# Layer 0 of a four-layer fp32 convolution net: who copies the expansion, when staged loads are used, and in what order the last convolution walks its cells

## The chip, the cores and the metric

The kernel runs on one core of one Trainium2 chip. The metric is the device time of one execution in microseconds (us), as the median of several runs. A difference below about 0.2% (14 us) can't be told from no change here.

## The reference, cut to what matters

Four layers, each of them `x + conv(group_norm(x))`, on `x` of shape (4, 64, 256, 256) in float32. Only layer 0 is changed:

```python
def _L0_conv_ref(x, w_in, w_dw, fft_filter, w_out):
    x = einsum('bchw,oc->bohw', x, w_in)               # 64 -> 384 channels (1x1)
    x = irfft2(rfft2(8x8 patches of x) * fft_filter)   # per channel, per patch
    x = depthwise_conv3x3(x, w_dw)                     # over patch borders
    x1, x2 = split(x, 2, axis=1)
    x = gelu(x1) * x2                                  # 192 channels
    return einsum('bchw,oc->bohw', x, w_out)           # 192 -> 64 channels (1x1)

x = x + _L0_conv_ref(_gn(x), ...)                      # _gn: group norm, 32 groups
```

## The kernel before, in words

**The mathematics.** The FFT filter on a patch and the 3x3 convolution after it are both linear and per channel, so the kernel turns them, for each channel, into one small matrix from the cells of a patch (and its right, lower and lower-right neighbours) to the cells of an output patch. These matrices are built once, at the start, and kept in DRAM (`wts`).

**The blocks.** The image is cut into 12 blocks `p` (4 images, 3 strips of 11 rows of patches each). A block is worked in four quarters `kb` of 96 channels. A quarter has these stages, in this order on TensorE (PE):

1. `expand(p, kb, t)` for 11 or 12 rows of patches `t`: 32 matmuls (64 rows in the trace, since each fp32 matmul is two instructions) of line 443 write one PSUM tile `psu`. Three copies then move it to the SBUF tile `u`: ScalarE (ACT) copies 128 partitions (line 452), then 64 partitions go once by ACT and once by VectorE (DVE) in turn over `t` (line 454), then DVE copies 64 more (line 455). The two halves of `u` hold even and odd patches at shifted places: E1, O1 are the places of the even and odd patch columns on the lower 64 partitions, O2, E2 on the upper.
2. `unit()`: one of the eight projections `project(p - 1, r)` of the block before, the last 1x1 convolution. Its operand `g` was written to DRAM by the block before and is loaded by `load_unit`: one residual tile `r` (two DMAs), and tiles `g1` and `g6` in two halves (some 12 DMAs), all issued by SyncE (SP). 32 matmuls (64 rows of the trace) in lines 585 and 592 write a PSUM tile `po`; DVE adds it to the residual (599, 601), takes statistics (607), and GpSimd (POOL) stores it (611).
3. `convolve(p, kb, g)` for `g` = 0 to 11: matmuls of lines 486 and 495 read `u` and weights `w`, and write a PSUM tile `pc`. ACT applies gelu into a tile `h` (502), DVE multiplies by the other half (503), POOL stores `h` to DRAM (506). One tile `w` serves two convolutions. After `g` = 6 a second `unit()` comes.

All PSUM tiles of the layer (`psu`, `pc`, `po`) are four banks wide and take turns in two slots (`quad`).

**What sets the order.** Everything stands in a manual schedule: PE, DVE, ACT and SP execute in the order in which the code is written, each waiting on its own operands. So a load at SP that waits for a free buffer holds back every load written after it, and an instruction of DVE or ACT that waits for a load holds back the copies written after it.

**The staged loads.** Beside `w`, `g` and `r`, two more streams come through SP within the quarters:

- Quarters 0 to 2 load pieces of the next image for its group-norm statistics: `load_stats` after each `g` with `g % 3 == 2`, `next_stats` (two statistics instructions of DVE, line 322) after each `g` with `g % 3 == 1`. The tiles have a pool of two buffers (`l0st`).
- Quarter 3 loads the input rows of the next block: `load_x` for two rows ahead of the convolutions 0 and 1, then `normalize_x` (ACT, line 258) of row `k` after the convolution `k + 1`, followed by the load of row `k + 2`. This pool has two buffers too (`l0x`).

`load_w` (line 463) is called ahead of every second convolution for the tile three places on; its pool has four buffers. The tiles `h` have three.

**At the start** SP loads statistics pieces in a pool of seven, then seven input rows, then the weights `win`, `wo6`, `wo1` (lines 656 to 658), two more rows, three tiles `w`; the last rows follow in the loop that normalizes.

**The projection's operands.** A row of `g` (34 values) holds 17 even and 17 odd patch columns, one after the other. The output must have them interleaved. `moving` reads them interleaved (innermost step from E1 to O1 or back, count 2), for one output cell `q` per matmul, and `out` is contiguous:

```python
return bass.AP(tensor=g.tensor, offset=g.offset + lo * CW + o, ap=[g.ap[0], [CW, m], [1, 8], [step, 2]])
out = lambda q, s: po[halves[s], q // 2, n * (q % 2) : n * (q % 2 + 1)].rearrange(
    "p (i j x) -> p i j x", i=m, x=2)
```

Of the kernel before, what the change touches and what calls it, by code (L numbers as in the profile page):

```python
# [10 lines left out]
F32 = mybir.dt.float32  # L11
# [6 lines left out]
C = 64  # L18
HID = 192
# [102 lines left out]
class _Net:  # L122
# [154 lines left out]
    def _layer0(self, ctx, dst):  # L277
        tc, nc, a, B, H, W = self.tc, self.nc, self.a, self.B, self.H, self.W
# [18 lines left out]
        NR = 11  # L297
# [9 lines left out]
        NB, NI = len(blocks), len(blocks) // B  # L307

        cp = pool("l0c", 1)
        p_xn, p_x, p_st = pool("l0xn", NR + 1), pool("l0x", 2), pool("l0st", 2)  # L310
        p_w, p_h = pool("l0w", 4), pool("l0h", 3)
        dr = ctx.enter_context(tc.tile_pool(name="l0d", bufs=1, space=DRAM))
        p_g = ctx.enter_context(tc.tile_pool(name="l0g", bufs=2, space=DRAM))
        wts = [dr.tile([2, 64, 2, Q, NC], F32, name=f"wt{t}") for t in range(HID // C)]
# [101 lines left out]
        def load_x(row, p_x=p_x):  # L416
            b, i = row
            x0[row] = p_x.tile([128, P, HW2], F32, tag="x", name=f"x0_{b}_{i}")
            for s in range(2):
                nc.sync.dma_start(x0[row][halves[s]], a["x"][b, :, P * i : P * i + P, s * HW2 : (s + 1) * HW2])  # L420
# [13 lines left out]
        def expand(p, kb, t):  # L434

            b, i0 = blocks[p]
            ps = quad(f"psu_{p}_{kb}_{t}")
            xn = xns[b, i0 + t]
            for k in range(2):
                for m in range(4):  # L440
                    for s in range(2):
                        for odd in range(2):
                            nc.tensor.matmul(  # L443
                                ps[halves[1 - odd], 2 * s + k, 2 * PB * m : 2 * PB * (m + 1)],
                                xn[halves[s], 2 * (4 * k + m) + odd].rearrange("p r w -> p (r w)"),
                                win[halves[s], kb, PB * (1 - odd) : PB * (3 - odd)], start=True, stop=True,
                            )
            v = ps[:, :, 0 : 8 * PB].rearrange("p s (m c) -> p c s m", m=4)
            n = 4 * 4
            at = lambda h, o: u[h, :, t * CW + o : t * CW + o + n].rearrange("p c (s m) -> p c s m", s=4)  # L450
            first, second = v[:, 0:PB], v[:, PB : 2 * PB]
            nc.scalar.copy(at(slice(0, 128), 1), first)  # L452
            lo, hi = halves
            (nc.vector.tensor_copy if t % 2 else nc.scalar.copy)(at(hi, E2 + 1), second[lo])  # L454
            nc.vector.tensor_copy(at(lo, O1), second[hi])  # L455

        def load_w(j):

            p, k = divmod(j, HID // 8)
            if p >= NB:  # L460
                return
            w = wl[j] = p_w.tile([128, 2, 4, NC], F32, tag="w", name=f"w_{j}")
            nc.sync.dma_start(
                w, wts[k // 8][:, :, :, 4 * (k % 8) : 4 * (k % 8) + 4].rearrange("h i k c n -> (h i) k c n")
            )
# [96 lines left out]
        def project(p, r):  # L562

            b, i0 = blocks[p]
            lo, hi, j0, rr = rows_in(p, r)
            m = hi - lo
            po = quad(f"po_{p}_{r}")
            rt = rts.pop((p, r))
            n = m * 16

            def moving(g, q, s):
                d = q < 7
                o, step = (O1 + 8 * s, E1 + 1 - O1) if d else (E1 + 8 * s, O1 - E1)
                return bass.AP(
                    tensor=g.tensor, offset=g.offset + lo * CW + o, ap=[g.ap[0], [CW, m], [1, 8], [step, 2]]
                )

            out = lambda q, s: po[halves[s], q // 2, n * (q % 2) : n * (q % 2 + 1)].rearrange(
                "p (i j x) -> p i j x", i=m, x=2
            )  # L580
            for half in range(2):
                g1, g6 = loads.pop((p, r, half))
                for q in range(4 * half, 4 * half + 4):
                    for s in range(2):
                        nc.tensor.matmul(  # L585
                            out(q, s), wo1, moving(g1[:, q % 4], q, s), start=(q % 2 == 0), stop=False,
                            skip_group_check=True,
                        )
                for q in (0, 2, 1, 3):
                    for s in range(2):  # L590
                        k = q // 2
                        nc.tensor.matmul(  # L592
                            out(4 * half + q, s), wo6[halves[k]], moving(g6[halves[k], q % 2], 4 * half + q, s),
                            start=False, stop=True, tile_position=(k * C, s * C), skip_group_check=True,
                        )
            rv = rt.rearrange("p i (j w) -> p w (i j)", w=P)
            pv = po[:, :, 0 : 2 * n].rearrange("p b (k n) -> p b k n", k=2)
            v = rv[:, 1:7].rearrange("p (b k) n -> p b k n", k=2)
            nc.vector.tensor_add(v, v, pv[:, 0:3])  # L599
            v = bass.AP(tensor=rv.tensor, offset=rv.offset + 7, ap=[rv.ap[0], [-7, 2], rv.ap[2]])  # L600
            nc.vector.tensor_add(v, v, pv[:, 3])  # L601
            if b not in bst1:
                bst1[b] = (self.stats_tile(f"bst1_{b}", 72), count())
            bst, slot = bst1[b]
            for k in range(0, m, 4):
                v = rt[:, k : min(k + 4, m)].rearrange("p i w -> p (i w)")
                nc.vector.bn_stats(bst[:, next(slot), :], v)
            if p % NI == NI - 1 and r == P - 1:
                self.norms.append(self.group_norm_parts(1, b, bst))
            for s in range(2):  # L610
                nc.gpsimd.dma_start(xr(dst[b])[rr][:, j0 : j0 + m, s * HW2 : (s + 1) * HW2], rt[halves[s]])  # L611

        def load_stats(b, j):
            t = st[b, j] = p_st.tile([128, 4, W], F32, tag="st", name=f"st{b}_{j}")
            for s in range(2):
                nc.sync.dma_start(t[halves[s]], src_t[b, :, j, s])

# [12 lines left out]
        with ordered:  # L630
# [6 lines left out]
            def first_stats(k):  # L637
# [2 lines left out]
                t = parts[k] = p_s.tile([128, 4, W], F32, tag="x", name=f"st_{k}")  # L640
                nc.sync.dma_start(t.rearrange("p r w -> p (r w)"), flat[:, 4 * W * k : 4 * W * (k + 1)])

            for k in range(7):
                first_stats(k)
            copies = [nc.scalar.copy, nc.gpsimd.tensor_copy, nc.scalar.copy]
# [6 lines left out]
            rows = rows_of(0)  # L652
            for row in rows[:7]:
                load_x(row, p_s)
            for s in range(2):
                nc.sync.dma_start(win[halves[s]], a["w_in"].rearrange("c (k n) -> c k n", k=4))
                nc.sync.dma_start(wo6[halves[s]], a["w_out"][128:HID])
            nc.sync.dma_start(wo1, a["w_out"][0:128])
            for row in rows[7:9]:
                load_x(row)  # L660
            for j in range(3):
                load_w(j)
            self.group_norm(0, 0, bst0, avgs)
            for k, row in enumerate(rows):
                normalize_x(row)
                if 7 <= k < 9:
                    load_x(rows[k + 2])
            ctx_a.close()

            p_1, p_6 = (pool(n, 2, side="right") for n in ("l0g1", "l0g6"))  # L670
# [13 lines left out]
            for p in range(NB + 1):  # L684
# [32 lines left out]
                for kb in range(4):  # L717
                    for t in range(NR + 1):
                        if 0 <= i0 + t < NP:
                            expand(p, kb, t)  # L720
                    unit()
                    for g in range(NG):
                        G = NG * kb + g
                        if g % 2 == 0:
                            load_w(p * (HID // 8) + G // 2 + 3)
                        if kb == 3 and g < 2 and g < len(fresh):
                            load_x(fresh[g])
                        convolve(p, kb, g)
                        self.next_norms()
                        if g == NG // 2:  # L730
                            unit()
                        if kb < 3:
                            if g % 3 == 2 and nk:
                                k = nk.pop(0)
                                load_stats(b + 1, k)
                                loaded.append(k)
                            if g % 3 == 1 and loaded:
                                next_stats(b + 1, loaded.pop(0))
                        else:
                            for k in loaded[:1]:  # L740
                                next_stats(b + 1, loaded.pop(0))
                            if 0 <= g - 1 < len(fresh):
                                k = g - 1
                                normalize_x(fresh[k])
                                if k + 2 < len(fresh):
                                    load_x(fresh[k + 2])
                for row in rows:
                    if row not in after:
                        xns.pop(row)
# [726 lines left out]
```

## Time and profile before

| | |
|---|---|
| median of 3 runs | 6848.48 us (6843.42 to 6849.02) |
| the profiled execution, its own time | 6848.19 us |
| span of its instructions | 6846.4 us |
| mean granted TensorE clock | 0.943 |
| PE busy | 5944.0 us, 87% |
| DVE busy | 3941.4 us, 58% |
| ACT busy | 2907.2 us, 42% |
| layer 0 (first `psu` matmul to last `po` matmul) | 114.5 to 4286.2 us |
| DMA, mean over the span | 212 GB/s |

How to read it. The profile holds one execution. Every row of its timeline is an instruction with its start, its length, its engine and its source line, the tiles written and read, and, in brackets, how long the engine had been idle before it and which event ended the idle time. PEld is the load of the stationary operand, which runs beside PE. SPq is a DMA issue. A table of windows gives, for a stretch of time, the busy time of each engine, the clock granted to PE, the share of 16 DMA engines in use, and GB/s. [...]

### The profile page before, as it was taken

The page shows a single profiled execution, that of the slowest core. Times are in us where ns is not written, and L with a number is a line of the kernel's source. Part 1 is how long each engine was busy: PE and PEld are TensorE (multiplying, and loading weights), DVE is VectorE, ACT ScalarE, POOL GpSimd, SP SyncE. Part 2 cuts the span into 40 slices and gives each one's busy share as a digit, 9 for nine tenths or more (in the row PEclk, how much of TensorE's full clock was granted, in tenths as well). Part 3 has the DMA queues.
Part 4 walks back from the last instruction along what each step waited for, and adds up shares of the span by engine and source line. Part 5 has one row for each costly group of instructions (what it writes and reads, how often), then busy time and mean ns, then how long its engine had stood idle before and what let it go on. Part 6 is the DMA issues. An engine that isn't in the chain of part 4 may idle for free.

```text
span 6846.4 us, 251669 instructions
## 1 busy us (share of the span) xinstructions
PE 5944.0 (87%) x115416; PEld 3058.7 (45%) x115416; DVE 3941.4 (58%) x4164; ACT 2907.2 (42%) x2900; POOL 1049.2 (15%) x1646
## 2 busy tenths in 40 slices
PE   2888888888888888888888886999989999999988
PEld 1444444444444444444444443333344444444476
DVE  5445444445444545444444343899878889886355
ACT  3333323232323233323333330677777788774211
POOL 3111111111111111111111111111112222221011
PEclk9999999999999999999999997999999999999855
DMA  7477878687878787878676768999956667667889
GB/s 221 147 197 200 215 201 220 196 216 198 213 202 212 205 214 200 209 207 209 176 207 174 206 176 220 242 228 228 230 132 174 171 175 176 176 168 253 333 342 395
DMA packets 878550, 1448.53 MB, mean 212 GB/s; under 512 B 77252, under 2 KB 586452, under 8 KB 875444
## 3 DMA queue, kind: packets, MB, share of 16 engines
q1 hardware_dynamic: 725284, 923.09, 53.4%
q0 software_dynamic: 148672, 500.14, 22.0%
q8 instruction: 908, 14.88, 1.0%
q10 hardware_dynamic: 3536, 9.20, 0.5%
q14 instruction: 150, 1.23, 0.1%
HBM read 932.08 MB, written 500.04 MB: 209 GB/s over the span
## 4 chain that ended last, share of the span: by engine, by line
PE 65%; DMA 13%; issue 7%; DVE 6%; ACT 5%; SPq 2%; POOL 1%; ACTq 0%; DVEq 0%; POOLq 0%
PE pc L495 12%; PE m L861 10%; PE pc L486 8%; PE one L1102 8%; PE psu L443 7%; PE div L1061 6%; DMA x<-in_x_dram 4%; PE po L585 4%; DVE u L455 3%; ACT u L452 3%; DMA g<-g 3%; DMA st<-in_x_dram 2%; PE psz L1091 2%; PE po L592 2%; DMA x<-x 2%
## 5 line engine op out<-in xcount | busy, mean ns | idle before, releaser
L443 PE MATMUL psu<-win,xn 64*64 64x96 f32 x34816 | 912.0, 258 | 507.3 <-DVE u L455 309.2
L503 DVE TENSOR_TENSOR h<-h,pc 128x748 f32<-128x748 f32 x576 | 536.2, 931 | 1248.5 <-ACT h L502 1248.4
L495 PE MATMUL pc<-u,w 64*16 64x374 f32 (+2 forms) x27648 | 1248.0, 484 | 0.0
L502 ACT ACTIVATE h<-pc 128x748 f32<-128x748 f32 x576 | 456.5, 793 | 1808.4 <-PE pc L495 1673.6
L443 PEld LDWEIGHTS psu<-win,xn 64*64 64x64 f32 x34816 | 825.2, 143 | 616.2 <-ACT u L452 203.9
L486 PE MATMUL pc<-u,w 64*64 64x374 f32 x9216 | 894.4, 497 | 81.4 <-DVE h L503 73.0
L495 PEld LDWEIGHTS pc<-u,w 64*16 64x16 f32 (+2 forms) x27648 | 413.8, 92 | 772.5 <-issue 772.3
L452 ACT COPY u<-psu 128x768 f32<-128x768 f32 x544 | 461.9, 849 | 665.1 <-PE psu L443 664.0
L506 POOL DMA_DIRECT2D g<-h x576 | 416.2, 723 | 1797.9 <-DVE h L503 1665.2
L258 ACT ACTIVATE xn<-x,nb,r 128x1024 f32<-128x1024 f32 (+3 forms) x272 | 486.4, 1791 | 459.7 <-DMA x<-in_x_dram 313.5
L455 DVE COPY u<-psu 64x768 f32<-64x768 f32 x544 | 521.7, 959 | 247.5 <-ACT u L454 238.0
L1047 DVE TENSOR_TENSOR q<-xn 128x2313 f32<-128x2313 f32 (+2 forms) x256 | 628.0, 2496 | 1.7 <-ACT xn L258 1.7
L1102 PE MATMUL one<-z,wp 32*32 32x512 f32 x16384 | 592.4, 596 | 19.1 <-issue 14.3
L486 PEld LDWEIGHTS pc<-u,w 64*64 64x64 f32 x9216 | 324.2, 134 | 588.4 <-issue 447.4
L1048 ACT ACTIVATE q<-q 128x2313 f32<-128x2313 f32 (+2 forms) x256 | 528.9, 2086 | 32.2 <-DVE q L1047 31.2
L1061 PE MATMUL div<-q,ones 64*32 64x512 f32 x8192 | 466.2, 594 | 13.6 <-ACT q L1048 9.3
L1102 PEld LDWEIGHTS one<-z,wp 32*32 32x32 f32 x16384 | 367.4, 103 | 225.9 <-issue 84.8
L454 DVE COPY u<-psu 64x768 f32<-64x768 f32 x272 | 258.9, 952 | 328.1 <-ACT u L452 327.1
L585 PE MATMUL po<-g,wo 128*64 128x176 f32 (+1 forms) x3072 | 360.1, 380 | 91.9 <-DMA g<-g 50.6
L1135 POOL DMA_DIRECT2D x<-r x512 | 274.5, 544 | 971.9 <-DVE r L1132 956.3
L611 POOL DMA_DIRECT2D x<-r x192 | 148.5, 778 | 1785.8 <-DVE r L601 1192.3
L599 DVE TENSOR_TENSOR r<-r,po 128x1056 f32<-128x1056 f32 (+1 forms) x96 | 197.3, 2055 | 367.4 <-PE po L592 335.6
(155 smaller groups left out, 6042.1 us busy)
## 6 DMA issues: line engine op xcount, KB each, us to landing
g<-h POOLq DMA_DIRECT2D x576, 374.0 KB, 7.3
x<-x SPq DMA_DIRECT2D x240, 640.0 KB, 6.5
w<-wt SPq DMA_DIRECT2D x288, 448.0 KB, 7.6
x<-x SPq DMA_DIRECT2D x100, 1024.0 KB, 14.1
g<-g SPq DMA_DIRECT2D x414, 187.0 KB, 5.7
g<-g SPq DMA_DIRECT2D x736, 93.5 KB, 5.5
x<-in_x_dram SPq DMA_DIRECT2D x256, 256.0 KB, 7.3
x<-o POOLq DMA_DIRECT2D x128, 512.0 KB, 8.3
```

Of the source, the lines that this page charges most:

```text
L443: nc.tensor.matmul(ps[halves[1 - odd], 2 * s + k, 2 * PB * m : 2 * PB * (m + 1)], xn[halves[s], 2 * (4 * k + m) + odd].rearrange("p r w -> ...
L452: nc.scalar.copy(at(slice(0, 128), 1), first)
L455: nc.vector.tensor_copy(at(lo, O1), second[hi])
L486: nc.tensor.matmul(out(C * c, C, k, h), w[halves[h], k, 2 * (G % 2) + c, 0:C], cells(h, 4 * g + 2 * k + c, 0, 0), start=True, stop=False, ...
L495: nc.tensor.matmul(out(q, m, k, h), w[halves[h], k, 2 * (G % 2) + c, c0 : c0 + m], cells(h, 4 * g + 2 * k + c, down, right), start=False, ...
L503: nc.vector.tensor_mul(h, h, v[:, 1])
L585: nc.tensor.matmul(out(q, s), wo1, moving(g1[:, q % 4], q, s), start=(q % 2 == 0), stop=False, skip_group_check=True,)
L861: nc.tensor.matmul(rows2(m)[halves[j], s], w[dx][halves[s]], ts[n][halves[s], i, 2 * j : 2 * j + 2, dx : dx + W], start=(dx == 0), stop=(d ...
L1047: nc.vector.tensor_sub(d, p0, p1)
L1048: nc.scalar.activation(d, d, AF.Square)
L1061: ins = nc.tensor.matmul(ps[quarters[j], h], ones[halves[h]], q[n, g, k][halves[h], r + 2 * j : r + 2 * j + 2, o : o + W], start=(m == 0), ...
L1102: ins = nc.tensor.matmul(rows2(ps[g])[quarters[j], k], w[quarters[i]], z[quarters[i], h, 2 * j + dy : 2 * j + dy + 2, dx : dx + W], tile_p ...
```

## The change

Six edits, all in layer 0.

1. The third copy of `expand` is no longer done in turn: ACT copies 28 of 48 channels, DVE the other 20, after DVE's own copy.
2. The pools: input rows and statistics pieces share one pool of four buffers; `w` has three buffers and is loaded two places ahead; `h` has four buffers.
3. Statistics pieces are loaded at `g % 3 == 0` and used two loads later.
4. Input rows of the next block: four are loaded at the end of quarter 2, each further one after the normalization of the row four before it.
5. In `project`, a matmul takes the cells of one parity `x` (even or odd patch columns) of two output cells `q`: its operand is read in runs of eight contiguous values and its output has step 2 in PSUM. The number of matmuls and their sizes stay.
6. At the start, the weights are loaded ahead of the first statistics pieces, four input rows follow the first seven at once, and two tiles `w` are loaded instead of three.

```diff
-        p_xn, p_x, p_st = pool("l0xn", NR + 1), pool("l0x", 2), pool("l0st", 2)
-        p_w, p_h = pool("l0w", 4), pool("l0h", 3)
+        p_xn, p_x = pool("l0xn", NR + 1), pool("l0x", 4)
+        p_w, p_h = pool("l0w", 3), pool("l0h", 4)
...
             nc.scalar.copy(at(slice(0, 128), 1), first)
             lo, hi = halves
-            (nc.vector.tensor_copy if t % 2 else nc.scalar.copy)(at(hi, E2 + 1), second[lo])
+            k = PB * 7 // 12
+            nc.scalar.copy(at(hi, E2 + 1)[:, 0:k], second[lo, 0:k])
             nc.vector.tensor_copy(at(lo, O1), second[hi])
+            nc.vector.tensor_copy(at(hi, E2 + 1)[:, k:], second[lo, k:])
...
-            def moving(g, q, s):
-                d = q < 7
-                o, step = (O1 + 8 * s, E1 + 1 - O1) if d else (E1 + 8 * s, O1 - E1)
+            def moving(g, bank, s, x):
+                at = lambda q: (O1 + 8 * s, E1 + 1 + 8 * s)[x] if q < 7 else (E1 + 8 * s, O1 + 8 * s)[x]
+                o, d = at(2 * bank), at(2 * bank + 1) - at(2 * bank)
                 return bass.AP(
-                    tensor=g.tensor, offset=g.offset + lo * CW + o, ap=[g.ap[0], [CW, m], [1, 8], [step, 2]]
+                    tensor=g.tensor, offset=g.offset + lo * CW + o, ap=[g.ap[0], [L + d, 2], [CW, m], [1, 8]]
                 )
 
-            out = lambda q, s: po[halves[s], q // 2, n * (q % 2) : n * (q % 2 + 1)].rearrange(
-                "p (i j x) -> p i j x", i=m, x=2
-            )
+            out = lambda bank, s, x: po[halves[s], bank, 0 : 2 * n].rearrange(
+                "p (q i j x) -> p x q i j", q=2, i=m, x=2
+            )[:, x]
             for half in range(2):
                 g1, g6 = loads.pop((p, r, half))
-                for q in range(4 * half, 4 * half + 4):
-                    for s in range(2):
-                        nc.tensor.matmul(
-                            out(q, s), wo1, moving(g1[:, q % 4], q, s), start=(q % 2 == 0), stop=False,
-                            skip_group_check=True,
-                        )
-                for q in (0, 2, 1, 3):
-                    for s in range(2):
-                        k = q // 2
-                        nc.tensor.matmul(
-                            out(4 * half + q, s), wo6[halves[k]], moving(g6[halves[k], q % 2], 4 * half + q, s),
-                            start=False, stop=True, tile_position=(k * C, s * C), skip_group_check=True,
-                        )
+                for k in range(2):
+                    for x in range(2):
+                        for s in range(2):
+                            nc.tensor.matmul(
+                                out(2 * half + k, s, x), wo1, moving(g1[:, 2 * k], 2 * half + k, s, x),
+                                start=(x == 0), stop=False, skip_group_check=True,
+                            )
+                for x in range(2):
+                    for k in range(2):
+                        for s in range(2):
+                            nc.tensor.matmul(
+                                out(2 * half + k, s, x), wo6[halves[k]],
+                                moving(g6[halves[k], 0], 2 * half + k, s, x),
+                                start=False, stop=True, tile_position=(k * C, s * C), skip_group_check=True,
+                            )
...
-            t = st[b, j] = p_st.tile([128, 4, W], F32, tag="st", name=f"st{b}_{j}")
+            t = st[b, j] = p_x.tile([128, 4, W], F32, tag="x", name=f"st{b}_{j}")
...
+            for s in range(2):
+                nc.sync.dma_start(win[halves[s]], a["w_in"].rearrange("c (k n) -> c k n", k=4))
+                nc.sync.dma_start(wo6[halves[s]], a["w_out"][128:HID])
+            nc.sync.dma_start(wo1, a["w_out"][0:128])
             for k in range(7):
                 first_stats(k)
...
-            for s in range(2):
-                nc.sync.dma_start(win[halves[s]], a["w_in"].rearrange("c (k n) -> c k n", k=4))
-                nc.sync.dma_start(wo6[halves[s]], a["w_out"][128:HID])
-            nc.sync.dma_start(wo1, a["w_out"][0:128])
-            for row in rows[7:9]:
+            for row in rows[7:11]:
                 load_x(row)
-            for j in range(3):
+            for j in range(2):
                 load_w(j)
             self.group_norm(0, 0, bst0, avgs)
             for k, row in enumerate(rows):
                 normalize_x(row)
-                if 7 <= k < 9:
-                    load_x(rows[k + 2])
...
                         if g % 2 == 0:
-                            load_w(p * (HID // 8) + G // 2 + 3)
-                        if kb == 3 and g < 2 and g < len(fresh):
-                            load_x(fresh[g])
+                            load_w(p * (HID // 8) + G // 2 + 2)
                         convolve(p, kb, g)
                         self.next_norms()
                         if g == NG // 2:
                             unit()
                         if kb < 3:
-                            if g % 3 == 2 and nk:
-                                k = nk.pop(0)
-                                load_stats(b + 1, k)
-                                loaded.append(k)
-                            if g % 3 == 1 and loaded:
-                                next_stats(b + 1, loaded.pop(0))
-                        else:
-                            for k in loaded[:1]:
-                                next_stats(b + 1, loaded.pop(0))
-                            if 0 <= g - 1 < len(fresh):
-                                k = g - 1
-                                normalize_x(fresh[k])
-                                if k + 2 < len(fresh):
-                                    load_x(fresh[k + 2])
+                            if g % 3 == 0:
+                                if len(loaded) == 2 or not nk:
+                                    for k in loaded[: 1 if nk else 2]:
+                                        next_stats(b + 1, loaded.pop(0))
+                                if nk:
+                                    k = nk.pop(0)
+                                    load_stats(b + 1, k)
+                                    loaded.append(k)
+                            if kb == 2 and g == NG - 1:
+                                for row in fresh[:4]:
+                                    load_x(row)
+                        elif 0 <= g - 1 < len(fresh):
+                            k = g - 1
+                            normalize_x(fresh[k])
+                            if k + 4 < len(fresh):
+                                load_x(fresh[k + 4])
```

## The prediction

> **What bounds the kernel now.** I read the page first (shares and costliest groups), then the waits, then the timeline of layer 0, stage by stage, and the table of windows over the same stages.
>
> ```profile
> PE 5944.0 (87%) x115416; PEld 3058.7 (45%) x115416; DVE 3941.4 (58%) x4164; ACT 2907.2 (42%) x2900; POOL 1049.2 (15%) x1646
> L443 PE MATMUL psu<-win,xn 64*64 64x96 f32 x34816 | 912.0, 258 | 507.3 <-DVE u L455 309.2
> ...
> L585 PE MATMUL po<-g,wo 128*64 128x176 f32 (+1 forms) x3072 | 360.1, 380 | 91.9 <-DMA g<-g 50.6
> ```
>
> PE is the engine to follow; in layer 0 its idle time (507 us) lies ahead of the expansion's matmuls. The start-to-start times of PE's rows in the timeline give the stages: over the 48 quarters the expansions take 1425 us, the convolutions 2168, the 88 projections within the loop 465 (5.44 us each with 176 columns, 4.99 with 160), the eight at the end 114.
>
> The expansion is bound by its copies (timeline, one slot's round):
>
> ```profile
> 863.05 1.55 PE L443 MATMUL psu<-win,xn 64*64 64x96 f32 x64 [0.51 <-DVE u L455]
> ...
> 864.71 0.85 ACT L452 COPY u<-psu 128x768 f32<-128x768 f32 x1 [0.38 <-PE psu L443]
> ...
> 865.59 0.95 DVE L454 COPY u<-psu 64x768 f32<-64x768 f32 x1 [0.28 <-ACT u L452]
> 866.56 0.96 DVE L455 COPY u<-psu 64x768 f32<-64x768 f32 x1
> ```
>
> The copies of one PSUM tile don't overlap: each starts some 0.03 us after the one before it ends, also across engines (in even `t`, DVE's L455 at 864.36 was released by ACT's L454). A round is matmul, three copies in series, next matmul (867.66): 4.61 us with DVE's third copy, 4.38 with ACT's. Two slots make that about 2.3 us per `t` against 1.55 of matmul.
>
> On top come loads that in-order engines wait for:
>
> ```profile
> ACT xn L258 <- DMA x<-in_x_dram: 277.2, 89, 10.5
> ...
> ACT h L502 <- DMA g<-h: 133.5, 39, 6.3
> ...
> DVE bst L322 <- DMA st<-in_x_dram: 116.0, 37, 6.7
> ```
>
> These are the waits within the loop. How such a wait reaches PE (timeline, quarter 3 of block 2): ACT sits at a normalization, the gelu behind it is late, DVE's product is late, and PE has no slot:
>
> ```profile
> 1079.30 1.24 ACT L258 ACTIVATE xn<-x,nb,r 128x1024 f32<-128x1024 f32 x1 [4.79 <-DMA x<-in_x_dram]
> 1080.44 0.77 ACT L502 ACTIVATE h<-pc 128x748 f32<-128x748 f32 x1
> ...
> 1081.25 0.93 DVE L503 TENSOR_TENSOR h<-h,pc 128x748 f32<-128x748 f32 x1 [5.78 <-ACT h L502]
> 1082.23 1.04 PE L585 MATMUL po<-g,wo 128*64 128x176 f32 x8 [1.83 <-DVE h L503]
> ```
>
> The windows of an expansion, its seven convolutions, and the seven of a quarter 3 (after the clock: DMA share, GB/s):
>
> ```profile
> 848.60:876.85 28.25, 19.81 (x712) 17.35 (x705) 16.47 (x18) 13.84 (x17) 0.72 (x1) 0.94 0.36 101
> ...
> 882.29:906.93 24.64, 24.64 (x452) 8.73 (x444) 12.46 (x15) 4.77 (x6) 5.99 (x8) 1.00 1.02 285
> ...
> 1048.24:1082.23 33.99, 28.62 (x456) 9.84 (x448) 10.75 (x16) 9.28 (x10) 5.84 (x8) 0.90 1.01 244
> ```
>
> Seven convolutions take 24.6 us (3.52 each) with PE never idle, 34.0 where rows are normalized. The DMA engines are full during convolutions and a third busy during expansions.
>
> [...] The trace shows the copies one after the other. [...] 16 rows of L585 take 1.80 us from their start to L592's, two column halves side by side, so 1.28 ns per column, and L592 (0.98 us, four side by side) 1.39. Runs of 17 (L486, 1.46 us for 16 rows, four side by side) take 0.98. [...] No matmul of this trace writes PSUM with a step. [...] fp32 here gives one column per 0.98 ns[...].
>
> **The change part by part.**
>
> *Copies (edit 1).* The two new copies aren't in the trace. ACT from PSUM: 512 elements 589 ns (L1294), 1024 in 1031 (L1095), so 448 in 0.53 us. DVE: 768 in 955, one element 153 (L209), so 320 in 0.49. The round becomes 1.55 + 0.11 + 0.85 + 0.02 + 0.53 + 0.04 + 0.96 + 0.02 + 0.49 + 0.1 = 4.67: the slower of the two of before. The order of the built program keeps DVE's first copy behind ACT's second. Load is balanced, but a series is not shortened: 0 to 0.08 us per `t`, 544 of them. I take **+10** (-20 to +45).
>
> *Projection (edit 5).* At 1.0 ns per column: 32 rows x 176/2 + 32 x 176/4 = 4.2 us instead of 5.44; 3.8 instead of 4.99. About 1.15 x 88 = **-100**. At 0.95: -125. If the stepped output costs: nothing gained[...]. The eight at the end wait for g<-g (88% of the chain there) and gain nothing. DVE's reads of `po` don't change.
>
> *Input rows (edits 2, 4).* In blocks 1 to 10, quarter 3's twelve convolutions exceed 12 x 3.53 us by 109 us in all; the expansions after it exceed the later ones by 43 in 11 blocks. The lead grows from two convolutions (7 us, landing 7.3 median) to four (14 us, less 3.6 for gelu, normalization and two issues at 0.64). The first four rows (8 issues, 5.1 us of SP, two each) go ahead of the projection's loads; those can't start until the projection, 28 us of expansion later, which hides them. But DMA is full in quarter 3, and only 4 of 11 rows leave it: I take **-80** and **-20** of 152 (-40 to -140). ACT has room: 0.77 + 1.24 in 3.52.
>
> *Statistics (edit 3).* Quarters 1 to 3 take 2.61 us per `t` in blocks 1 to 8, 2.41 in blocks 9 to 11, which load none: 0.2 x 11.3 x 24 = 55; **-50** (-20 to -60), as each piece is now 21 us old when used. Their two DVE instructions (1.28 us) are hidden beside 0.93 per convolution, except after `g` = 6, behind the projection's additions: 2.12 + 0.80 + 1.75 + 1.28 + 0.93 = 6.9 against two convolutions, 7.0: **+5** (0 to 10). Their two DMAs stay behind a `load_w` each.
>
> *Fourth `h`.* ACT's 133 us of waits reach PE in block 0 alone (12 convolutions in 45 to 47 us instead of 42.3): **-12** (-15 to 0). No POOL instruction moves.
>
> *Third `w` buffer gone.* The load ahead of `g` = 0 serves `g` = 4 instead of 6. It stands at SP behind the projection's loads:
>
> ```profile
> 887.21 2.81 SPq L463 DMA_DIRECT2D w<-wt  x2
> ...
> 896.34 1.52 PE L486 MATMUL pc<-u,w 64*64 64x374 f32 x16
> ```
>
> Issued at 887.21, landed at 896.66; `g` = 4 starts at 896.34. Setting each such load's landing against that convolution: late in 29 of 33 (blocks 1 to 11, quarters 0 to 2), 46 us in all, 1.4 each, so 61 for 44 quarters; a shorter projection brings the convolution, not SP's chain of issues, forward by 0.55: **+80** (0 to 130). PE waits, and all behind it. At other `g` the margin is positive (`g` = 2 for 6: median 3.5 us).
>
> *Start (edit 6).* Five weight issues (3.5 us) leave the place between input rows and go ahead of the statistics pieces. ACT's first copy (131.67) waited for rows landing at 130; the first matmul was at 114.5. **-6** (-10 to +3).
>
> Sum: +10 - 100 - 80 - 20 - 50 + 5 - 12 + 80 - 6 = -173. From the profiled execution's 6848.2 (median 6848.5, the same): **6675 us**. Its own range, with each unknown half way to its bounds: 6610 to 6740.
>
> **The rivals.**
> A. The `w` loads land in time and the rows are hidden: -80 for `w` and -25 for rows on top: 6570. For: expansions leave DMA two thirds free. Against: the 29 late landings.
> B. The convolutions become DMA-bound (share 1.02 already): rows give -40, `w` costs 130, so +110: 6785.
> C. The stepped PSUM output costs what the hops cost: 6775.
> D, the slower side: [...] The other parts sum to -73, so it decides once a projection takes 5.28 + 73/88 = 6.1 us (1.5 ns per column). [...]
> E. Small gains, eaten by new waits: within 0.2% (what a measurement of this kernel can tell from no change), 6848. That edit 1 doesn't do what it says is in the forecast already.
>
> **How the numbers follow.** Forecast 0.50, A 0.15, B 0.12, C 0.10, D 0.10, E 0.03. Faster: the first four, 0.87; same 0.03; slower 0.10. The range leaves out D, E and the far edge of A: 6560 to 6800.
>
> **What would show it.** PE's start-to-start of a projection: 4.2 us (right), 5.4 (C), over 6.1 (D). Rounds of the expansion still 4.6 us, with DVE's first copy released by ACT's second. No `bst L322 <- st` wait; `xn L258` waits under 100 us. PE idle ahead of L486 at `g` = 4 waiting for w<-wt, 1 to 2 us per quarter; if absent, A. Expansions near 2.4 us per `t`. It is wrong if copies of one tile overlap, or PE waits for loads at other convolutions.

## The result, and the profile after

The changed kernel takes **6868.13 us** (median of 20 runs, 6849.46 to 6895.68), the kernel before 6850.27 (20 runs, 6840.27 to 6872.78): a ratio of 1.0025 (95% interval 1.0014 to 1.0036). It is slower by a quarter of a per cent, where the prediction had 6675 us. The profiled execution took 6889.14 us, 21 us above the median of its runs, with a span of 6887.4. Layer 0 ends at 4311.1 us instead of 4286.2. The other 16 us lie in layers whose code is the same, so only what lies in layer 0 is explained here.

The page, first shares and costliest groups; the line numbers have moved by two to four (L488 was L486, L456 was L455, and L455 and L457 are the two parts of the shared copy):

```profile
PE 5931.4 (86%) x115416; PEld 3078.3 (45%) x115416; DVE 3944.2 (57%) x4436; ACT 2973.2 (43%) x3172; POOL 1049.0 (15%) x1646
L443 PE MATMUL psu<-win,xn 64*64 64x96 f32 x34816 | 934.2, 260 | 495.1 <-DVE u L457 303.6
...
L488 PE MATMUL pc<-u,w 64*64 64x374 f32 x9216 | 896.9, 498 | 119.3 <-DMA w<-wt 88.8
...
L588 PE MATMUL po<-g,wo 128*64 128x176 f32 (+1 forms) x3072 | 315.3, 348 | 97.1 <-DMA g<-g 56.9
```

The projection's group is shorter (315.3 us, before 360.1), but the expansion's idle time has hardly moved (495.1, before 507.3), and the convolutions' first group has an idle time of 119.3 us with a releaser that the page of before did not name: the weights `w`.

The waits within the loop tell what was swapped for what. First the kernel before (us in total, times, longest):

```profile
PE psu L443 <- DVE h L503: 122.4, 51, 6.0
...
PE pc L486 <- DVE h L503: 73.0, 25, 7.3
PE psu L443 <- issue: 34.4, 36, 4.2
```

and after:

```profile
PE psu L443 <- issue: 101.6, 72, 4.4
PE pc L488 <- DMA w<-wt: 88.8, 39, 5.3
...
DVE bst L322 <- DMA st<-in_x_dram: 27.0, 6, 5.2
PE psu L443 <- DVE h L505: 24.1, 39, 3.2
PE pc L488 <- DVE h L505: 23.6, 15, 2.0
```

The stalls that the staged loads caused are gone: PE's waits for `h` fell from 122.4 + 73.0 to 24.1 + 23.6, by 148 us. In their place stand two others: "issue" (PE waits for none of the events in the profile) rose by 67 us, and the wait for `w` is new with 89. Together 156. ACT's waits for input rows at L258, 277.2 us before, are wholly gone in the loop.

By stages of PE (start to start, layer 0, us; the few matmuls of the group norm, about 20 us in all, are counted with the convolutions):

| | expansions (48) | convolutions | projections | layer 0 ends |
|---|---|---|---|---|
| before | 1424.6 | 2168.1 | 579.0 | 4286.2 |
| after | 1451.2 | 2241.1 | 513.8 | 4311.1 |

So -65 in the projections, +73 in the convolutions, +27 in the expansions; the first expansion also starts 9.5 us earlier, but is 9.6 longer, so the start gives nothing. For the other expansions the table leaves +17. PE's wait for `h` is 98 us shorter, "issue" 67 longer, the waits for copies of `u` 19 (311 to 330), the projection's waits for the expansion ahead of it some 10, and line 443 is busy 23 us longer (890.3 to 913.1 in the loop): together +21, near enough.

**The wait for `w`**, in the timeline of block 2, quarter 2:

```profile
978.34 0.56 SPq L465 DMA_DIRECT2D w<-wt  x1
978.39 1.52 PE L488 MATMUL pc<-u,w 64*64 64x374 f32 x16
...
985.34 2.77 PE L488 MATMUL pc<-u,w 64*64 64x374 f32 x16 [3.36 <-DMA w<-wt]
988.04 3.74 PE L497 MATMUL pc<-u,w 64*16 64x374 f32 x48
```

and the windows before, during and after it (PE, PEld, DVE, ACT and POOL busy; clock, DMA share, GB/s):

```profile
978.40:981.90 3.50, 3.50 (x72) 1.25 (x64) 0.93 (x1) 0.79 (x1) 0.72 (x1) 1.00 1.00 296
981.90:985.30 3.40, 0.09 (x8) 0.00 (x0) 2.13 (x3) 0.79 (x1) 0.71 (x1) 0.90 1.03 240
985.30:991.70 6.40, 6.36 (x64) 1.83 (x64) 0.00 (x0) 0.00 (x0) 0.00 (x0) 0.52 1.04 319
```

The load leaves SP one convolution before it is needed, PE waits 3.36 us, and then the convolution itself takes 6.4 us instead of 3.5, at a granted clock of 0.52 where the one before the wait had 1.00. Here the loss after the wait is nearly as large as the wait. Mostly it is smaller, and it comes after shorter waits too: none of after's 19 waits for `w` under 2 us was followed by a slower convolution (clock 1.00 over each), but 18 of the 20 from 2.29 us up were (clock 0.52 to 0.71), by 1.3 to 2.9 us each, 33 us in all. That second loss is not in the waits, and comes on top of their 88.8. Summed over blocks 1 to 11, the intervals of `g` = 3 and 4 (wait and slow convolution together) exceed 3.52 us each by 117 us in quarters 0 to 2 and by 136 with quarter 3.

**The "issue" waits.** Block 7, quarter 3, the third pair of tiles of the expansion:

```profile
2768.72 0.55 PE L443 MATMUL psu<-win,xn 64*64 64x96 f32 x13 [1.28 <-DVE u L457]
2772.78 4.52 PE L443 MATMUL psu<-win,xn 64*64 64x96 f32 x115 [3.52 <-issue]
```

PE stops in the middle of a tile, 13 rows into it, with every operand there. The trace also holds each packet of the queue that the DMA view names "instruction" (q8, 16 KB each). In after's expansions they come 4.7 us apart (median), about one round of two tiles, which is 256 rows of PE and PEld; over the whole execution 909 packets stand against 230,832 such rows, 254 a packet. The DMA view of the stretch ahead of this wait, and then of the next 2 us:

```profile
q1 hardware_dynamic: 2088, 1.04, 86.8%
q0 software_dynamic: 165, 0.53, 27.5%
```

```profile
q1 hardware_dynamic: 761, 0.38, 118.8%
q8 instruction: 1, 0.02, 4.3%
```

For 6 us (2763.5 to 2769.5) the loads fill the 16 engines (86.8% + 27.5%) and no instruction packet comes; one then ends at 2771.17, and PE goes on 1.6 us later. The same holds for all of them: each of the 67 "issue" pauses over 0.3 us in after's expansions (100.4 us), and each of the 30 in before's (33.0 us), ends within 2 us of the end of an instruction packet, eight in ten of them 1.3 to 1.6 us after it. So they are read here as waits of PE for its own instructions. (That reading is the author's, from these times and the 254 rows a packet: whose packets they are, and when PE asked for one, the trace does not show.) Sorted by how full the DMA engines were in the 5 us ahead of the packet's end: under 0.3, at most one of some 140 packets of after's expansions held PE up; over 0.9, about two thirds of some 85. Before has about as many packets over 0.9, but fewer than three in ten held PE up. A likely reason, read from the waits and not tested: there PE stood at the expansion's start anyway, for the copies behind a late statistics piece, and the packet had the time. That PE goes on late where the packet comes late, and mostly with the engines full, is what this trace shows, by the counts above.

### The profile page after: what moved, and what is told of

The parts are those of the page before. It is cut to its first block, busy times and chain, and to the rows that moved or that the text cites. A ratio compares the mean times of both kernels' runs of the same rounds, so it can differ in the third digit from the quotient of the medians.

```text
span 6887.4 us, 252749 instructions
## 1 busy us (share of the span) xinstructions
PE 5931.4 (86%) x115416; PEld 3078.3 (45%) x115416; DVE 3944.2 (57%) x4436; ACT 2973.2 (43%) x3172; POOL 1049.0 (15%) x1646
## 4 chain that ended last, share of the span: by engine, by line
PE 66%; DMA 14%; ACT 6%; DVE 5%; issue 5%; SPq 4%; POOL 0%; ACTq 0%; DVEq 0%; POOLq 0%
PE pc L497 13%; PE m L863 10%; PE pc L488 9%; PE psu L443 8%; PE one L1104 8%; PE div L1063 6%; DMA w<-wt 4%; DMA g<-g 4%; PE po L588 3%; ACT u L452 3%; DMA x<-x 2%; PE psz L1093 2%; SPq L544 2%; PE po L595 2%; ACT u L455 2%
## 5 line engine op out<-in xcount | busy, mean ns | idle before, releaser
L443 PE MATMUL psu<-win,xn 64*64 64x96 f32 x34816 | 934.2, 260 | 495.1 <-DVE u L457 303.6
L497 PE MATMUL pc<-u,w 64*16 64x374 f32 (+2 forms) x27648 | 1263.1, 489 | 0.7 <-issue 0.7
L443 PEld LDWEIGHTS psu<-win,xn 64*64 64x64 f32 x34816 | 842.5, 144 | 606.8 <-issue 254.0
L488 PE MATMUL pc<-u,w 64*64 64x374 f32 x9216 | 896.9, 498 | 119.3 <-DMA w<-wt 88.8
L456 DVE COPY u<-psu 64x768 f32<-64x768 f32 x544 | 522.0, 960 | 687.7 <-ACT u L455 637.5
L488 PEld LDWEIGHTS pc<-u,w 64*64 64x64 f32 x9216 | 325.4, 134 | 623.8 <-issue 483.8
L258 ACT ACTIVATE xn<-x,nb,r 128x1024 f32<-128x1024 f32 (+3 forms) x272 | 485.5, 1788 | 180.9 <-DMA x<-x 142.8
L588 PE MATMUL po<-g,wo 128*64 128x176 f32 (+1 forms) x3072 | 315.3, 348 | 97.1 <-DMA g<-g 56.9
L863 PE MATMUL m<-t,wk 64*64 64x512 f32 x3072 | 341.1, 588 | 0.0
```

The source lines that it names most:

```text
L443: nc.tensor.matmul(ps[halves[1 - odd], 2 * s + k, 2 * PB * m : 2 * PB * (m + 1)], xn[halves[s], 2 * (4 * k + m) + odd].rearrange("p r w -> ...
L488: nc.tensor.matmul(out(C * c, C, k, h), w[halves[h], k, 2 * (G % 2) + c, 0:C], cells(h, 4 * g + 2 * k + c, 0, 0), start=True, stop=False, ...
L497: nc.tensor.matmul(out(q, m, k, h), w[halves[h], k, 2 * (G % 2) + c, c0 : c0 + m], cells(h, 4 * g + 2 * k + c, down, right), start=False, ...
L588: nc.tensor.matmul(out(2 * half + k, s, x), wo1, moving(g1[:, 2 * k], 2 * half + k, s, x), start=(x == 0), stop=False, skip_group_check=True,)
L863: nc.tensor.matmul(rows2(m)[halves[j], s], w[dx][halves[s]], ts[n][halves[s], i, 2 * j : 2 * j + 2, dx : dx + W], start=(dx == 0), stop=(d ...
```

## The experiments

Theory, once the traces were compared: (1) the third `w` buffer costs far more than the +80 predicted; (2) the gains of the staged loads are taken back by the instruction waits; (3) the shared copy costs more than +10. Rivals: the projection gained nothing because its stepped output is slow; the loss lies in the copies alone; or the loads filled the DMA, so that `w` would be late with any buffers. All ratios are against the kernel before on the same chip, with the 95% interval.

**1. The projection alone** (edit 5 put into the kernel before).

```diff
-ap=[g.ap[0], [CW, m], [1, 8], [step, 2]]
+ap=[g.ap[0], [L + d, 2], [CW, m], [1, 8]]
...
-"p (i j x) -> p i j x", i=m, x=2
+"p (q i j x) -> p x q i j", q=2, i=m, x=2
```

> The kernel before with the new projection alone. Stage ledger theory: the 88 projections inside the loop take 4.67 and 4.28 us instead of 5.44 and 4.99, nothing gives that back, so 65 us less than before: about 6785 us, ratio 0.990. Rival (the convolutions are bound by DMA, so PE's saved time comes back as waits of the convolutions): less than 25 us saved, and PE waits ahead of L486 or L443 grow by 40 us or more.

Measured: 0.9946 (0.9931 to 0.9961), 37 us of the 65 expected, so between theory and rival. The stage gains what it gains in after (579.0 to 512.8), but the convolutions go from 2168.1 to 2182.8: the extra time lies in quarter 3. The likely reason is that the rows of the next block, which come no earlier, take the time back.

**2. The shared copy alone** (edit 1 put into before).

```diff
-(nc.vector.tensor_copy if t % 2 else nc.scalar.copy)(at(hi, E2 + 1), second[lo])
+k = PB * 7 // 12
+nc.scalar.copy(at(hi, E2 + 1)[:, 0:k], second[lo, 0:k])
...
+nc.vector.tensor_copy(at(hi, E2 + 1)[:, k:], second[lo, k:])
```

> The kernel before with the shared third copy alone. Series theory (three copies in series, now four, a round of two tiles 4.77 instead of 4.62 us): 25 to 40 us more than before, about 6880 us, ratio 1.005. Rival (load balance of ACT and DVE sets the pace): a gain or no change, rounds at or under 4.6 us.

Measured: 1.006 (1.0045 to 1.0074), +41 us; expansions +32. The median round of two tiles is 4.71 us, before 4.62.

**3. After, with four `w` buffers and three `h`**, as before.

```diff
-p_w, p_h = pool("l0w", 3), pool("l0h", 4)
+p_w, p_h = pool("l0w", 4), pool("l0h", 3)
...
-load_w(p * (HID // 8) + G // 2 + 2)
+load_w(p * (HID // 8) + G // 2 + 3)
```

> The changed kernel with four buffers for w, loaded three places ahead again, and three for h. Late-w theory: the stalls at g = 4 and the slow clock after them, some 115 us in the blocks 1 to 11, go; h waits in block 0 come back with about 6: about 6760 us, ratio to before 0.987. Rival (DMA is full, whatever PE does not wait for at g = 4 it waits for elsewhere): 6830 us or more, with new waits ahead of L488 at other g.

Measured: 0.9854 (0.9835 to 0.9872), close to what was expected. In the profile layer 0 is 138 us shorter than after's, 137 of it in the convolutions (2241.1 to 2104.2). PE's waits:

```profile
PE psu L443 <- issue: 101.5, 69, 3.8
...
PE pc L488 <- DVE h L505: 16.0, 11, 1.9
```

No wait for `w` is left, and the one for instructions is what it was. That ACT waits for free `h` again (196.4 us) reaches PE nowhere.

**4. The staging alone** (after with copies and projection of before: edits 2, 3, 4 and 6).

```diff
-nc.scalar.copy(at(hi, E2 + 1)[:, 0:k], second[lo, 0:k])
-nc.vector.tensor_copy(at(hi, E2 + 1)[:, k:], second[lo, k:])
+(nc.vector.tensor_copy if t % 2 else nc.scalar.copy)(at(hi, E2 + 1), second[lo])
```

> The changed kernel with the copies and the projection of before: loads and buffers alone. Ledger theory: what the loads lose (convolutions at g = 3 and 4, the last statistics pieces, expansions of quarter 3) is more than what they win (63 us of quarter 3, 23 of the first expansions): 20 to 55 us more than before, 6870 to 6905 us. The stall at g = 4 should be shorter than in the changed kernel by about 0.5 us each, as the longer projection leaves SP more time. Rival (the loads are a gain and the copies the loss): under 6840 us.

Measured: 0.9967 (0.9952 to 0.9982), some 23 us less than before. The main expectation, 20 to 55 us more, was wrong, and its rival held: the loads are a gain. PE's waits:

```profile
PE psu L443 <- issue: 96.7, 65, 3.3
...
PE pc L486 <- DMA w<-wt: 62.1, 36, 4.1
```

The instruction waits thus come with the loads, whoever copies. Still the expansions take 1387.9 us, 37 less than before, and 63 less than after. As the projection alone leaves them where they were (1425.4 in experiment 1), the shared copy costs about 63 us of expansions on top of the staged loads, twice what it costs alone (experiment 2). `w` is late by 1.7 us a time instead of 2.3: with the longer projection (5.44 us instead of 4.67) the convolution that needs it comes later; SP's chain of issues does not. The parts don't simply add: -37 (projection), +41 (copies) and -23 (loads) make -19, where after has +17.

**5. The third copy always by ACT**, in the kernel before: less balanced, but the shorter series.

```diff
-(nc.vector.tensor_copy if t % 2 else nc.scalar.copy)(at(hi, E2 + 1), second[lo])
+nc.scalar.copy(at(hi, E2 + 1), second[lo])
```

> The kernel before with the third copy always at ACT (which has 1.65 us of copies per t then, DVE 0.96). Series theory: only the sum of the three copies counts, 0.85 + 0.80 + 0.96 instead of 0.95 in every second t, so every round of two tiles is 4.38 us instead of 4.62: up to 0.12 us per t, 30 to 65 us less than before, ratio about 0.993. Rival (the more loaded engine sets the pace): no gain or a loss, rounds of 4.6 us or more.

Measured: 0.9938 (0.9919 to 0.9957), expansions 1378.9 us (-46). Its round in the timeline, first of one slot, from matmul to matmul 4.39 us:

```profile
855.38 3.25 PE L443 MATMUL psu<-win,xn 64*64 64x96 f32 x128 [1.51 <-DVE u L455]
...
857.05 0.85 ACT L452 COPY u<-psu 128x768 f32<-128x768 f32 x1 [1.02 <-PE psu L443]
...
857.93 0.80 ACT L454 COPY u<-psu 64x768 f32<-64x768 f32 x1
...
858.76 0.96 DVE L455 COPY u<-psu 64x768 f32<-64x768 f32 x1 [1.74 <-ACT u L454]
...
859.77 1.46 PE L443 MATMUL psu<-win,xn 64*64 64x96 f32 x59 [1.15 <-DVE u L455]
```

Against it, the series of four in after (one slot from its matmul to its last copy):

```profile
958.44 1.55 PE L443 MATMUL psu<-win,xn 64*64 64x96 f32 x64 [1.23 <-DVE u L457]
...
960.11 0.85 ACT L452 COPY u<-psu 128x768 f32<-128x768 f32 x1 [1.38 <-PE psu L443]
...
960.98 0.53 ACT L455 COPY u<-psu 64x448 f32<-64x448 f32 x1
961.54 0.96 DVE L456 COPY u<-psu 64x768 f32<-64x768 f32 x1 [1.32 <-ACT u L455]
...
962.52 0.48 DVE L457 COPY u<-psu 64x320 f32<-64x320 f32 x1
```

In both each copy waits for the one before it. (Whether it has to was not tried: the second and third copies read different halves of the partitions of `psu`.) 0.80 of one copy became 0.53 + 0.48 of two and one more handover; the median round is 4.40 here, 4.62 before, 4.71 in experiment 2.

**6. The projection with a contiguous PSUM output** (experiment 1, its output columns in another order, so that PSUM is written without a step).

```diff
-"p (q i j x) -> p x q i j", q=2, i=m, x=2
+"p (x q i j) -> p x q i j", q=2, i=m, x=2
```

> The kernel before with the new projection, whose output is written contiguously: even and odd columns are not interleaved, so the layer's output has its columns in another order. If the stepped output is what keeps the projection at 4.67 us, it falls to 4.2 to 4.3, some 35 us less than p_only. If the reads in runs of eight are, it stays at 4.67 and the time is that of p_only.

Measured: 0.9933 (0.9914 to 0.9951). One projection, the last line being the next convolution:

```profile
880.44 1.60 PE L586 MATMUL po<-g,wo 128*64 128x176 f32 x16 [0.74 <-issue]
881.97 0.93 PE L593 MATMUL po<-g,wo 64*64 64x176 f32 x16
882.83 1.59 PE L586 MATMUL po<-g,wo 128*64 128x176 f32 x16
884.36 0.92 PE L593 MATMUL po<-g,wo 64*64 64x176 f32 x16
885.09 1.46 PE L486 MATMUL pc<-u,w 64*64 64x374 f32 x16
```

4.65 us, where after has 4.67 with step 2 (963.21 to 967.88); all projections of the layer take 511.5 us here and 512.8 in experiment 1. The stepped output costs nothing that can be measured here, and the prediction's rivals C and D fall: C, by which the step costs what the interleaved reads of before cost, kept a projection at 5.4 us, and D, with the step slower still, took it over 6.1.

**7. Three `w` buffers and four `h` in the kernel before**, nothing else.

```diff
-p_w, p_h = pool("l0w", 4), pool("l0h", 3)
+p_w, p_h = pool("l0w", 3), pool("l0h", 4)
...
-load_w(p * (HID // 8) + G // 2 + 3)
+load_w(p * (HID // 8) + G // 2 + 2)
```

> The kernel before with three buffers for w loaded two places ahead, and four for h: nothing else. Late-w theory: each quarter's convolution 4 waits for its w, 1 to 3 us[...]: 50 to 110 us more than before, less some 10 for block 0: ratio about 1.010. Rival (the wait is absorbed by the row loads of quarter 3 and the slack of the copies): within 20 us of before.

Measured: 1.0065 (1.0046 to 1.0084), +45 us, at the low end of what was expected; the convolutions go to 2224.8. Alone, the edit costs 32.0 us of waits for `w`, a third of after's 88.8. So the price of one edit hangs on the others.

**8. After with four `w` buffers and without the stream of statistics pieces** (the statistics of images 1 to 3 are those of one resident piece; input rows then have three buffers).

```diff
+            if "one" not in st:
+                st["one"] = cp.tile([128, 4, W], F32, name="st_one")
...
+            st[b, j] = st["one"]
```

> w_back without the traffic of the statistics pieces: one piece is loaded once and used for all, so the statistics of the images 1 to 3 are those of one piece; DVE's work stays, the rows have three buffers instead of four. It asks what the idle time of PE inside the expansions is that the profile puts to issue (2.2 to 2.6 us per expansion in blocks 1 to 8 of w_back, 0.2 to 0.6 before). If the loads in flight slow PE's supply of instructions: 1.3 us or less in quarters 1 and 2. If it is that PE no longer stands still at the second tile: 2 us or more, as in w_back. The stall at the last convolution of quarter 2 goes in either case (28 us in all).

Measured: 0.9778 (0.9757 to 0.9799), layer 0 37 us shorter than in experiment 3. In blocks 1 to 11 the instruction waits fall where pieces were in flight: quarter 1 from 22.5 to 16.7 us, quarter 2 from 22.6 to 6.8. In quarters 0 and 3, where input rows and the projection's loads are, they rise, from 29.4 to 34.3 and from 22.9 to 32.3. So the test is clear for quarter 2 alone (0.4 us per expansion in blocks 1 to 8); quarter 1, with 1.6, lies between the two marks set, and the sum of these waits hardly falls. The last convolution of quarter 2 exceeds its 3.52 us by 6.9 in all, against 28.5 in experiment 3: there the last piece was late.

**9. Three buffers, but the load of `w` for `g` = 4 issued ahead of the projection's loads.**

```diff
+                    load_w(p * (HID // 8) + NG * kb // 2 + 2)
                     unit()
...
-                        if g % 2 == 0:
+                        if g % 2 == 0 and g > 0:
```

> The changed kernel with one line moved: the load of w ahead of convolution 0 of each quarter is issued ahead of the projection's loads instead of behind them; three buffers for w and four for h stay. Queue theory (the tile is late because it stands behind the projection's issues at SP): the stalls at g = 3 and 4 and the slow clock after them go, 115 to 140 us, ratio to before 0.983 to 0.986, as in w_back. Rival (two places of lead are too few, or DMA is full): more than 50 us of stalls remain at g = 4, or come at g = 6, ratio over 0.992.

Measured: 0.9893 (0.988 to 0.9907), short of what was expected, and better than the rival. The place in SP's queue removes the stalls as the buffer does (waits for `w` 2.0 us; convolutions 2102.2 against 2104.2 in experiment 3). But the load now stands in the expansion, and the expansions take 1491.2 us against 1456.1. Its waits:

```profile
PE psu L443 <- issue: 123.6, 85, 4.8
```

**10. Experiment 9 with the copies of experiment 5 and the statistics pieces two at the first place**, so that the last is old enough too.

```diff
-                                if nk:
+                                for k in nk[: 2 if kb == 0 and g == 0 else 1]:
```

> w_early with the third copy always at ACT, and the statistics pieces loaded one place earlier (two at the first place), so that the last one too is two places old when it is used. If the parts add up: w_back's 0.9854, less 83 us for the copies (c_only against act3), less 26 for the last piece: ratio 0.969, about 6640 us. If the gains share the same waits: 0.978 or more.

**11. The same two edits on experiment 3** (four `w`, three `h`).

> The same two edits on w_back (four buffers for w, three for h) instead of w_early. It should be within 15 us of best_e, on its slow side by the h waits of block 0 (some 6 us).

Measured: 0.9764 (0.9747 to 0.9781) for 10 and **0.972** (0.9706 to 0.9733) for 11, 6659.18 us against 6855.62. Neither expectation was met. 10 lies between its two marks (0.969 and 0.978), nearer to the second, so the gains do share waits in part. 11, expected within 15 us of 10 and on its slow side, is faster by 35: the buffer is better than the earlier issue, and the difference is again in the expansions (1419.1 against 1382.3). PE's waits of 11:

```profile
PE psu L443 <- DVE u L455: 262.9, 327, 1.5
...
PE psu L443 <- issue: 116.2, 72, 3.8
```

Waits for statistics and for `w` are gone from the list, and PE's for `h` are down to 34 us; what is left in the expansion is the series of copies and the "issue" waits.

## Why the prediction was wrong

The step that failed is the one called **"Third `w` buffer gone"**, at +80 (0 to 130). Beside it "Copies" was mis-sized, and a term is missing. By stages of PE the prediction's terms make -7 us for the convolutions, -60 for the expansions, -100 for the projections and -6 for the start; the profiles show +73, +27, -65 and -9.5 (9.6 of the +27 only take back the earlier start).

- **`w`: +80 became 117 to 138.** (Experiment 3 gives back 1.0025 - 0.9854, or 117 us, by the ratios and 138 in the profile.) That the load behind the projection's loads would be late at `g` = 4 was right, with its place, and the waits themselves, 88.8 us, are near the +80. The shorter projection was counted too, at 0.55 us of lateness. But the waits were priced at their length only: the slower convolutions after 18 of them add 33 us. And the lateness was read from a trace in which the other loads stood elsewhere: alone the edit costs 45 us (experiment 7), with the other loads 62 of waits (4), with the shorter projection and the shared copy too 89 (after).
- **PE's instructions: no term.** The prediction had nothing for "issue" in the expansion, and read the DMA engines as two thirds free there. As a mean that is so (share 0.36 in its window of an expansion); at the start of an expansion they can be full (share 1.14 from 2763.5 to 2769.5), and of the packets in after's expansions that ended behind 5 us with a share over 0.9, about two thirds held PE up. It seems that the start stall that edits 2 to 4 removed had covered that: the first pair of tiles of an expansion (mean of blocks 1 to 8, quarters 1 to 3) went from 7.0 to 7.4 us down to 4.9 to 5.4 (experiments 3 and 4), and 67 us came back as instruction waits, 62 of them with the loads alone (experiment 4). So the -70 for rows and statistics in the expansions became -37 there.
- **Statistics, -50:** right for the stall at the start, which is gone; given back as said. "Each piece is now 21 us old" was wrong for the last piece of a quarter 2, which is used one place after its load, behind the projection's loads: DVE's six waits of 27.0 us, and +24 us at the last convolution.
- **Rows, -80 and -20:** the convolutions of quarter 3 exceed 3.52 us by some 61 us instead of some 121, so -60, with a late `w` among what is left; the expansions of quarter 0 are 23 us shorter, those of quarter 3, where rows now stand, 24 longer.
- **Projection, -100:** right in kind, -65 in the stage. 16 rows of L588 take 1.54 us and of L595 0.86, so 1.09 and 1.22 ns per column, not the 1.0 assumed. That the output's step costs nothing was the author's estimate, and it held (experiment 6: 511.5 us without the step, 512.8 with it in experiment 1). Whether the rest lies with the reads was not tried apart.
- **Copies, +10:** right in kind, as the copies are a series; mis-sized. The new copies take 0.53 and 0.48 us as estimated, but the round of two tiles becomes 4.71 us instead of 4.67, and the expansions lose 32 us alone (experiment 2) and about 63 on top of the staged loads (experiment 4), more than the +45 given as the far end. Half of those 63 are rows of line 443 that take longer (882.3 us in experiment 4, 913.1 in after), 12 are waits for copies. The granted clock over the expansions is lower too (0.927 in after, 0.944 in experiment 4; over the whole execution 0.938 and 0.945). What lowers it stays open: not the instruction waits alone, since experiment 4 has nearly as many and its rows are shorter than before's 890.3.
- **Fourth `h`, -12:** block 0's convolutions exceed by some 10 us instead of some 15. **Start, -6:** nothing. **After `g` = 6, +5:** nothing to see.

Rival A was wrong, as `w` was late; B had the price of `w` (130) right, but kept the other gains; E, "small gains, eaten by new waits", comes nearest, at 0.03, though it named neither wait. A lesson on chances: each gain was a wait removed, and that several waits are replaced at once had only this 0.03.

## What to carry to other kernels

Before a stall is taken away, look at what it covers: the next thing that arrives in that time may be a weight, a row, or, as the "issue" waits are read here, the engine's own instructions. A load has a place in SP's queue and a place in the DMA engines' traffic: moved ahead of the projection's loads (experiment 9), `w` cost PE 2.0 us of waits instead of 88.8, but the "issue" waits of the expansions went from 101.6 to 123.6. So full stretches should be looked at, not the mean share. And a wait of PE can cost more than its length: here 88.8 us of waits brought 33 more in slower convolutions. Last, a part measured alone is not its price beside the others: the shared copy cost 32 us in one setting and 63 in the other.

## What the runs showed of the hardware that was not expected

- The DMA traffic has an instruction queue (q8: 909 packets of 16 KB in after's execution, one for every 254 rows of PE and PEld), and every "issue" pause over 0.3 us of the expansion ended within 2 us of the end of such a packet (eight in ten 1.3 to 1.6 us after it). With the DMA engines over 0.9 busy in the 5 us before, about two thirds of the packets in after's expansions held PE up; under 0.3, at most one of some 140.
- In after, a convolution ran slower after 18 of the 20 waits for `w` from 2.29 us up, by 1.3 to 2.9 us at a granted clock of 0.52 to 0.71, and after none of the 19 under 2 us (clock 1.00).
- An fp32 matmul that writes PSUM with step 2 takes the time of a contiguous one (a projection of 4.67 us in after, 4.65 without the step; all of the layer 512.8 and 511.5). For this shape no run here shows a slowing.
- The better balanced copies lost 0.6%, and the worse balanced ones, shorter in series, won 0.6% (experiments 2 and 5).
